# A macaron block on one core: both turn orders of the attention loop written anew, and four kinds of side work moved from VectorE to ScalarE and GpSimd

## The chip, the cores and the metric

The kernel runs on one core of a Trainium2 chip. The metric is the device time of one execution in microseconds (us). The core's engines run at the same time, each through its own list of instructions, in order: TensorE (PE: matmuls and transposes, with its weight loads shown as PEld), VectorE (DVE), ScalarE (ACT), GpSimd (POOL) and SyncE (SP, which here only issues DMAs). They wait for each other on semaphores.

## What is computed

The input x has 2 batches of 1024 rows and 512 columns, all in float32. Three residual steps follow each other:

```python
x = x + 0.5 * ffn(layernorm(x), W_base, b_base, W_router, lora_A, lora_B)
x = x + attn(layernorm(x), q_weight, q_scale, ..., o_weight, o_scale)
x = x + 0.5 * ffn(layernorm(x), W_base, b_base, W_router, lora_A, lora_B)

def ffn(x):      # base layer, and a low-rank part: 8 experts of rank 16, the best 2 weighted
    w = weights of the top 2 of softmax(x @ W_router.T)
    h = einsum('td,erd->ter', x, lora_A)
    return x @ W_base.T + b_base + 2 * einsum('ter,eor,te->to', h, lora_B, w)

def bitnet_linear(x, weight, scale):
    s = max(mean(abs(weight), axis=1), 1e-8)
    y = (x @ sign(weight / s).T) * (s * scale)
    return nan_to_num(y, nan=0, posinf=1e6, neginf=-1e6)

def attn(x):     # 32 query heads of 16, 8 key and value heads
    q, k, v = bitnet_linear(x, ...) three times
    a = softmax(q @ k.T / 4)
    return bitnet_linear(a @ v, o_weight, o_scale)
```

## The kernel before

The attention is the trunk of the program. It is cut into 32 units (a batch, half of its 1024 queries, one of the 8 key heads with its 4 query heads), and a unit into 4 turns. One turn issues, for three units at different stages:

- m: 8 score tiles of 128 queries by 512 keys, two matmuls each (p = 0 and 1, line 742), and for each tile a row maximum on VectorE (`m_max`, line 751);
- e: 8 score tiles of 128 keys by 512 queries of an earlier unit, three matmuls each (lines 781 and 785; the third subtracts the maximum), and for each tile the exponential on ScalarE into one of 14 `es` buffers (line 787);
- A: four parts of the product of exponentials and values (`a_part`, line 820), one turn behind e. All parts of a unit add up in one PSUM bank, `av`, of which there is only one. After the unit's last part, `unit_end` has ScalarE copy `av` out (line 795).

An m or e matmul uses 32 of the array's 128 rows, those of its head, which is the tile's number modulo 4. Four that follow each other with four different heads run at once. The order of m, e and A in a turn is written by hand: `FULL` and `BARE` (line 663 on), and `LEAD_IN` for the first three turns. `e1(6)` means matmul p = 1 of e tile 6, `A2` part 2. Seven PSUM banks are shared by m tiles, e tiles and all the rest; the bank that has been free longest is taken first.

The rest (layer norms, both FFNs, projections) is written as "strands": Python generators that yield the engine and the wait of their next step. Nothing of this exists when the kernel runs; it only decides in which order the instructions are recorded. A turn counts as 64 ticks. At the slots `F`, `V`/`W`, `C`/`D` of the order a ready strand may record one step on TensorE (`P`), VectorE (`v`) or ScalarE (`a`), after every item one on GpSimd (`g`) and one on SyncE (`d`). `LATER` says how many ticks a step has to wait after the step that it depends on. A turn takes `FULL` when a P step will be ready by tick 40, else `BARE`, which has no `F`. One P step is, for example, one of four column chunks of an FFN base tile, four of the eight matmuls of an output tile, or four transposes. In the loop before, 97 turns are `FULL`, 32 `BARE` and 3 `LEAD_IN`. Before a unit's q and k are loaded (`place`) or its v is laid out (`place_v`), `need` makes sure that the projections which feed them have been recorded: it lets the strands record step after step, with no attention work between them, until they are there.

Steps that the change touches, while the attention runs (`flow.free` is False then; before and after the loop it is True):

- `finite` (line 227) replaces infinities and NaN: with `fast` = 0 GpSimd clamps (249, 253) and adds (255), VectorE makes the mask (251) and copies the finite values over (259).
- `ln_T` (267): GpSimd makes `rstd` (281), VectorE the normalized rows `xn` (288), TensorE transposes them, ScalarE copies.
- `ffn_tiles`, in it `base` (410): GpSimd makes `xb` = x + half the bias (414), TensorE adds up five chunks (419, 423), VectorE writes 0.5 times the sum plus `xb` to x (425); then the store, or the statistics of the next norm (`stats`, 264).
- `o_proj` (617): VectorE multiplies the projection by the scales (639), then `finite`, then GpSimd adds to x (645).

Of the kernel before, what the change touches and what calls it, by code (L numbers as in the profile page):

```python
# [8 lines left out]
F32 = mybir.dt.float32  # L9
# [3 lines left out]
ALU = mybir.AluOpType  # L13
AX = mybir.AxisListType

P = 128
# [16 lines left out]
def macaron_kernel(ctx: ExitStack, tc: tile.TileContext, x_in, wbT, b_base, wrT, aT, bT,  # L33
# [192 lines left out]
    def finite(y, o, n, fast, back):  # L226
# [20 lines left out]
        else:  # L247
            yield "g", src, t
            nc.gpsimd.tensor_scalar(lo_, y, 0.0, -BIG, ALU.min, ALU.max)  # L249
            yield "v", src, t  # L250
            nc.vector.tensor_scalar(m_, y, 0.0, 0.0, ALU.mult, ALU.is_equal)
# [18 lines left out]
    def ln_T(xt, n, mv, given, tiles, xs, rank):  # L270
# [10 lines left out]
        nc.gpsimd.tensor_tensor(rstd[:, own], ve[:, own], mhalf[:, own], ALU.pow)  # L281
        at = flow.t

        def part(t):
            yield "r", dict(t=1)
            yield "v", "g", at
            xn = t512(f"xn{n}_{t}")
            nc.vector.tensor_scalar(xn, xt[:, t, :], mv[:, t, 0:1], rstd[:, t:t + 1], ALU.subtract,
                                    ALU.mult)
            yield "P", "v", None, 1  # L290
            pt = bank(f"pt{n}_{t}").rearrange("p (c q) -> p c q", c=KC)
            for c in range(KC):
                nc.tensor.transpose(pt[:, c, :], xn[:, c * P:(c + 1) * P], ident)
            flow.give(t=1)
            yield "a", "P"
            tok = slice(t * P, (t + 1) * P)
            nc.scalar.copy(xT[:, :, tok], pt)
            if xL is not None:
                yield "v", "a"
                nc.vector.tensor_tensor(xL[:, :, tok], pt, xT[:, :, tok].bitcast(F32), ALU.subtract)  # L300
            flow.give(fb=1)
# [18 lines left out]
    def ffn_tiles(xt, name, rank, tiles, xT, hT, mv, given, mv2, summed, store, loads):  # L320
# [89 lines left out]
        def base(t):  # L410
            yield "r", dict(t=1)
            yield "g", ""
            xb = t512(f"xb{n}_{t}")
            nc.gpsimd.tensor_tensor(xb, xt[:, t, :], bh, ALU.add)
# [9 lines left out]
            yield "v", "P"  # L424
            nc.vector.scalar_tensor_tensor(xt[:, t, :], pb, 0.5, xb, ALU.mult, ALU.add)
            flow.give(t=1, fb=1)
            if store is not None:
                yield ("a" if flow.free else "d"), "v"
                (nc.scalar if flow.free else nc.sync).dma_start(store[t * P:(t + 1) * P, :],
                                                                xt[:, t, :])  # L430
            if mv2 is not None:
                yield "v", "v"
                stats(xt, t, mv2, n)
                summed.add(t)
# [184 lines left out]
    def o_proj(b, g, hs, rank, mv, given, fast=False):  # L619
# [5 lines left out]
        def part(t):  # L625
# [11 lines left out]
            yield "v", "P"  # L637
            y = t512(f"yo{n}_{t}")
            nc.vector.tensor_tensor(y, po, osc, ALU.mult)  # L639
            flow.give(fb=1)  # L640
            done.append(t)
            r = t512(f"ro{n}_{t}")
            yield from finite(y[:, :], r[:, :], f"o{n}_{t}", fast, ("v", flow.t))
# [8 lines left out]
        for t in range(TG):  # L652
# [10 lines left out]
    FULL = ("e0(3) e0(2) m0(5) m0(0) e1(3) e1(2) m1(5) V m1(0) e2(3) e2(2) C e0(1) A0 A1 A2 A3 S "  # L663
            "m0(1) m0(6) e0(7) e0(4) m1(1) m1(6) e1(7) W e1(4) e1(1) m0(2) e2(7) e2(4) e2(1) C "
            "m1(2) V F e0(6) e0(0) m0(7) e0(5) e1(6) e1(0) m1(7) e1(5) e2(6) e2(0) D m0(3) e2(5) "
            "m0(4) m1(3) F m1(4)")
    BARE = ("C m0(1) m0(2) e0(3) e0(4) V m1(1) e0(6) e1(3) e1(4) m0(5) e1(6) e2(4) e2(3) m1(5) "
            "m1(2) A0 S e2(6) e0(1) m0(0) e0(7) e1(1) C m1(0) e1(7) W m0(6) e2(1) e0(0) e2(7) m1(6) "
            "A1 e1(0) V m0(7) e0(5) e0(2) e2(0) D m1(7) e1(2) e1(5) m0(4) m0(3) e2(2) e2(5) m1(4) "
            "m1(3) A2 A3")  # L670
# [4 lines left out]
         for o in t.split()] for t in (FULL, BARE, LEAD_IN))  # L675
    TU = NT // 2
# [154 lines left out]
    def attention(chains, n0):  # L831
# [7 lines left out]
        def need(*keys):  # L839
            for _ in range(4000):  # L840
                flow.settle()
                if set(keys) <= ended:
                    return
# [6 lines left out]
        for n in range(n0, TU * len(units) + LEAD + 1):  # L850
# [8 lines left out]
            order = (LEAD_IN if not e and not a else FULL if flow.wants("P", begin + TICK * 5 // 8)  # L859
# [3 lines left out]
            for pos, (kind, p, i) in enumerate(order):  # L863
# [7 lines left out]
                elif kind == "A":  # L871
                    if a:
                        a_part(a[0], a[1] * 2 + p // 2, p % 2)
# [149 lines left out]
```

## Time and profile before

| | |
|---|---|
| median of 3 runs | 1261.95 us (1256.4 to 1266.83) |
| the profiled execution: time, span of its instructions | 1256.92 us, 1255.2 us |
| mean granted TensorE clock | 0.915 of full speed |
| the loop over turns, first matmul of its first turn to first matmul of its last | 118.4 to 1183.5 us |
| row maximum, line 751, VectorE | 1024 x 682 ns |
| exponential, line 787, ScalarE | 1024 x 599 ns |
| m matmuls, line 742; e matmuls, lines 781 and 785 | 2048 x 464 ns; 2048 x 474 ns and 1024 x 431 ns |
| A matmuls, line 820, each float32 one in two passes | 4096 x 416 ns |
| FFN base, line 419, the same | 256 passes, 68.9 and 64.8 us in all |

Durations of matmuls overlap, so their sum is not TensorE's time; what counts there is the distance from one start to the next. Each row of 40 digits on the page cuts the span in slices of 31.4 us; a digit is the busy share in tenths. Where `PEclk` has an 8 or a 7 the array ran at half speed for part of the slice.

### The profile page before, as it was taken

What the parts mean: (1) busy time and instruction counts of PE and PEld (TensorE: products, weight loads), DVE (VectorE), ACT (ScalarE), POOL (GpSimd) and SP (SyncE); (2) the same over time, 40 slices, a digit from 0 to 9 for tenths busy, and PEclk for the clock granted to TensorE, in tenths of its full rate; (3) what the DMA queues carried; (4) which work ended last, traced back from release to release, by engine and by line L of the source; (5) the groups of instructions that cost most, each with busy time, mean ns of one, the idle gap of its engine ahead of it and who ended that gap; (6) DMA issues with size and microseconds to landing.
All of it is one profiled execution on the core that took longest, in us unless ns stands there. A gap on an engine that the chain in (4) does not pass through costs nothing.

```text
span 1255.2 us, 25499 instructions
## 1 busy us (share of the span) xinstructions
PE 1148.8 (92%) x10501; PEld 606.1 (48%) x10501; DVE 902.8 (72%) x1733; ACT 641.6 (51%) x1249; POOL 295.0 (24%) x302
## 2 busy tenths in 40 slices
PE   3988699999999999999999999999999999998868
PEld 3546355454454544444554445444455444545434
DVE  5578876767786777776677976777769677895273
ACT  2222255655554665565565666455557655566401
POOL 3135832000000340031555220241000300422110
PEclk8989588899986999987999899899989899999788
DMA  7010332121212222223132241122222422211110
GB/s 254 1 59 34 81 122 85 52 52 52 52 52 52 69 80 57 70 76 89 49 90 75 72 122 53 33 52 69 61 60 67 123 68 65 68 55 38 45 39 34
DMA packets 38708, 85.57 MB, mean 68 GB/s; under 512 B 7728, under 2 KB 10800, under 8 KB 34624
## 3 DMA queue, kind: packets, MB, share of 16 engines
q1 hardware_dynamic: 37184, 81.26, 22.4%
q8 instruction: 82, 1.34, 0.4%
q10 hardware_dynamic: 1152, 2.10, 0.4%
q0 software_dynamic: 256, 0.59, 0.3%
q14 instruction: 34, 0.28, 0.1%
HBM read 59.57 MB, written 23.84 MB: 66 GB/s over the span
## 4 chain that ended last, share of the span: by engine, by line
PE 70%; DVE 19%; issue 3%; DMA 2%; POOL 2%; ACT 1%; SPq 1%; POOLq 0%; ACTq 0%; DVEq 0%
PE av L820 20%; PE m L742 16%; DVE mn L751 11%; PE e L781 10%; PE pbf L419 5%; PE pbs L419 5%; PE e L785 4%; PE po L634 2%; PE phs L342 1%; DMA qd<-y 1%; PE pq L504 1%; PE pbf L423 1%; PE pv L521 1%; PE pbs L423 1%; DMA x<-in_x 1%
## 5 line engine op out<-in xcount | busy, mean ns | idle before, releaser
L751 DVE TENSOR_REDUCE mn<-m 128x1 f32<-128x512 f32 x1024 | 657.0, 682 | 230.0 <-PE m L742 221.4
L787 ACT ACTIVATE es<-e 128x512 f32<-128x512 f32 x1024 | 546.9, 599 | 425.6 <-PE e L785 401.4
L742 PE MATMUL m<-k,q 32*128 32x512 f32 x2048 | 492.1, 464 | 21.1 <-DVE mn L751 15.1
L781 PE MATMUL e<-q,k 32*128 32x512 f32 x2048 | 407.9, 474 | 8.3 <-DVE mn L751 6.9
L742 PEld LDWEIGHTS m<-k,q 32*128 32x128 f32 x2048 | 240.8, 196 | 153.0 <-issue 67.4
L820 PE MATMUL av<-es,vaug 128*32 128x256 f32 x4096 | 290.3, 416 | 16.4 <-issue 10.3
L781 PEld LDWEIGHTS e<-q,k 32*128 32x128 f32 x2048 | 185.1, 194 | 114.7 <-DVE mn L751 69.6
L785 PE MATMUL e<-mq,ones_r 2*128 2x512 f32 x1024 | 233.0, 431 | 3.7 <-DMA mq<-mT 3.7
L820 PEld LDWEIGHTS av<-es,vaug 128*32 128x32 f32 x4096 | 121.5, 116 | 154.5 <-issue 103.8
L785 PEld LDWEIGHTS e<-mq,ones_r 2*128 2x128 f32 x1024 | 125.6, 196 | 25.1 <-issue 13.7
L419 PE MATMUL pbf<-wb,xTf 128*128 128x512 f32 x128 | 68.9, 653 | 1.3 <-DVE mn L751 1.3
L419 PE MATMUL pbs<-wb,xTs 128*128 128x512 f32 x128 | 64.8, 618 | 1.2 <-DVE mn L751 1.2
L586 POOL TENSOR_TENSOR an<-an,rb 128x512 f32<-128x512 f32 x15 | 19.2, 1281 | 142.7 <-DMA rd<-rs 72.1
L249 POOL TENSOR_SCALAR loa<-y 128x512 f32<-128x512 f32 x17 | 12.7, 750 | 157.1 <-ACT y L509 147.5
L726 POOL MEMSET vaug<- 128x128 f32 x32 | 6.6, 206 | 137.7 <-PE av L820 137.6
L419 PEld LDWEIGHTS pbf<-wb,xTf 128*128 128x128 f32 x128 | 23.2, 203 | 30.1 <-issue 26.1
L419 PEld LDWEIGHTS pbs<-wb,xTs 128*128 128x128 f32 x128 | 21.5, 189 | 27.1 <-issue 22.9
L253 POOL TENSOR_SCALAR z<-y 128x512 f32<-128x512 f32 x17 | 34.1, 2008 | 1.8 <-DMA qd<-y 0.6
L249 POOL TENSOR_SCALAR loo<-yo 128x512 f32<-128x512 f32 x12 | 7.4, 613 | 113.7 <-DVE yo L639 110.0
L537 POOL TENSOR_TENSOR z<-z,y 128x512 fp32r<-128x512 f32 x17 | 21.9, 1293 | 51.0 <-ACT y L534 51.0
L590 POOL TENSOR_TENSOR anxL<-an,anxT 128x512 fp32r<-128x512 f32 x15 | 19.2, 1280 | 53.5 <-ACT anxT L588 53.4
L634 PE MATMUL po<-sign_o,anxT 128*128 128x512 f32 x64 | 29.4, 459 | 1.2 <-DVE mn L751 1.2
(193 smaller groups left out, 1008.3 us busy)
## 6 DMA issues: line engine op xcount, KB each, us to landing
k<-kd SPq DMA_DIRECT2D x31, 1024.0 KB
q<-qd SPq DMA_DIRECT2D x32, 256.0 KB
ad<-avs SPq DMA_DIRECT2D x32, 256.0 KB
x<-in_x SPq DMA_DIRECT2D x16, 256.0 KB
qd<-y SPq DMA_DIRECT2D x16, 256.0 KB
qd<-z SPq DMA_DIRECT2D x16, 256.0 KB
an<-ad SPq DMA_DIRECT2D x15, 256.0 KB
rb<-rd SPq DMA_DIRECT2D x15, 256.0 KB
```

The costliest lines, as they stand in the source:

```text
L249: nc.gpsimd.tensor_scalar(lo_, y, 0.0, -BIG, ALU.min, ALU.max)
L253: nc.gpsimd.tensor_scalar(o, y, 0.0, BIG, ALU.max, ALU.min)
L419: nc.tensor.matmul(pb, xT[:, c, t * P:(t + 1) * P], wb[:, c, :], start=(c == 0), stop=False)
L423: nc.tensor.matmul(pb, hT[0][:, t * P:(t + 1) * P], lb, start=False, stop=True)
L537: (nc.vector if fast else nc.gpsimd).tensor_tensor(lo, o, y, ALU.subtract)
L634: nc.tensor.matmul(po, hs[j][:, c, t * P:(t + 1) * P], wo[:, c, :], start=(c + j == 0), stop=(c + j == KC))
L742: nc.tensor.matmul(s["m", i], s["q"][rows, qt * P:(qt + 1) * P], s["k"][rows, 1 - p, kh * 512:(kh + 1) * 512], start=(p == 0), stop=(p == 1))
L751: nc.vector.tensor_reduce(s["mn"][:, h, qt, kh:kh + 1], s.pop(("m", i)), AX.X, ALU.max, negate=True)
L781: nc.tensor.matmul(t, s["k"][rows, 1 - p, kt * P:(kt + 1) * P], s["q"][rows, :], start=(p == 0), stop=False)
L785: nc.tensor.matmul(t, ones_r[two, :], s["mq"][two, :], start=False, stop=True)
L787: nc.scalar.activation(e, s.pop(("e", i)), AF.Exp, scale=HD ** -0.5)
L820: nc.tensor.matmul(s["av"][32 * h:32 * h + 32, cols], s["v"][:, kt, :], s["es"][kt * REP + h][:, cols], start=(kt + half == 0), stop=(kt + ...
```

## The change

It does five things.

1. `FULL` and `BARE` are new orders of the same 44 attention items. In `FULL` the four A parts, which stood together at places 13 to 16 of 53, are now two pairs, one after the first eleven e and m items, one at the very end. In `BARE` they were one, one and two; now they are one, two and one, the last at the end. `at_F`, the tick by which a P step must be ready for `FULL` to be taken, goes from 40 to 36.
2. Before a unit's first A part, `until` now lets strands record steps until the copy of the previous unit's `av` has been recorded.
3. In `finite` with `fast` = 0 the mask (251) is made by GpSimd.
4. While the attention runs, `ln_T` makes `xn` on ScalarE from `rstd` and a new `neg` = -mean x rstd, for which GpSimd gets two small operations a group of tiles.
5. While the attention runs, FFN sums leave PSUM through a ScalarE copy with the factor 0.5 and are added to x by GpSimd, and output tiles leave through a ScalarE copy and are multiplied by the scales on GpSimd. The bias is now added to x in place in all cases.

Counted in the built program: VectorE loses 28 `xn`, 33 masks, 16 FFN sums and 12 scalings, 89 operations. ScalarE gains 28, 16 and 12, GpSimd 33, 16 and 12 of 128x512 and 16 of 128x4 or less. 91 turns are now `FULL`, 38 `BARE`, 3 `LEAD_IN`. The number of matmuls stays, and so does the number of DMAs.

```diff
@@ -247,8 +247,8 @@
         else:
             yield "g", src, t
             nc.gpsimd.tensor_scalar(lo_, y, 0.0, -BIG, ALU.min, ALU.max)
-            yield "v", src, t
-            nc.vector.tensor_scalar(m_, y, 0.0, 0.0, ALU.mult, ALU.is_equal)
+            yield "g", ""
+            nc.gpsimd.tensor_scalar(m_, y, 0.0, 0.0, ALU.mult, ALU.is_equal)
             yield "g", ""
             nc.gpsimd.tensor_scalar(o, y, 0.0, BIG, ALU.max, ALU.min)
             yield "g", "g"
@@ -279,15 +279,26 @@
         yield "g", "v"
         rstd = sm.tile([P, TG], F32, tag="rstd", name=f"rstd{n}{tiles[0]}", bufs=4)
         nc.gpsimd.tensor_tensor(rstd[:, own], ve[:, own], mhalf[:, own], ALU.pow)
+        calm = not flow.free
+        if calm:
+            yield "g", ""
+            neg = sm.tile([P, TG], F32, tag="neg", name=f"neg{n}{tiles[0]}", bufs=4)
+            nc.gpsimd.tensor_tensor(neg[:, own], mv[:, own, 0], rstd[:, own], ALU.mult)
+            yield "g", ""
+            nc.gpsimd.tensor_scalar(neg[:, own], neg[:, own], -1.0, None, ALU.mult)
         at = flow.t
 
         def part(t):
             yield "r", dict(t=1)
-            yield "v", "g", at
+            yield "a" if calm else "v", "g", at
             xn = t512(f"xn{n}_{t}")
-            nc.vector.tensor_scalar(xn, xt[:, t, :], mv[:, t, 0:1], rstd[:, t:t + 1], ALU.subtract,
-                                    ALU.mult)
-            yield "P", "v", None, 1
+            if calm:
+                nc.scalar.activation(xn, xt[:, t, :], AF.Identity, bias=neg[:, t:t + 1],
+                                     scale=rstd[:, t:t + 1])
+            else:
+                nc.vector.tensor_scalar(xn, xt[:, t, :], mv[:, t, 0:1], rstd[:, t:t + 1],
+                                        ALU.subtract, ALU.mult)
+            yield "P", "a" if calm else "v", None, 1
             pt = bank(f"pt{n}_{t}").rearrange("p (c q) -> p c q", c=KC)
             for c in range(KC):
                 nc.tensor.transpose(pt[:, c, :], xn[:, c * P:(c + 1) * P], ident)
@@ -410,8 +421,7 @@
         def base(t):
             yield "r", dict(t=1)
             yield "g", ""
-            xb = t512(f"xb{n}_{t}")
-            nc.gpsimd.tensor_tensor(xb, xt[:, t, :], bh, ALU.add)
+            nc.gpsimd.tensor_tensor(xt[:, t, :], xt[:, t, :], bh, ALU.add)
             for c in range(KC):
                 yield ("P", "P") if c else ("P", "", flow.t, 1)
                 if c == 0:
@@ -421,15 +431,24 @@
                 flow.lock = bs[t] if c < KC - 1 else None
             yield "P", "a", ready
             nc.tensor.matmul(pb, hT[0][:, t * P:(t + 1) * P], lb, start=False, stop=True)
-            yield "v", "P"
-            nc.vector.scalar_tensor_tensor(xt[:, t, :], pb, 0.5, xb, ALU.mult, ALU.add)
-            flow.give(t=1, fb=1)
+            if flow.free:
+                yield "v", "P"
+                nc.vector.scalar_tensor_tensor(xt[:, t, :], pb, 0.5, xt[:, t, :], ALU.mult, ALU.add)
+                flow.give(t=1, fb=1)
+            else:
+                yield "a", "P"
+                hb = t512(f"hb{n}_{t}")
+                nc.scalar.activation(hb, pb, AF.Copy, scale=0.5)
+                flow.give(fb=1)
+                yield "g", "a"
+                nc.gpsimd.tensor_tensor(xt[:, t, :], xt[:, t, :], hb, ALU.add)
+                flow.give(t=1)
             if store is not None:
-                yield ("a" if flow.free else "d"), "v"
+                yield ("a" if flow.free else "d"), "v" if flow.free else "g"
                 (nc.scalar if flow.free else nc.sync).dma_start(store[t * P:(t + 1) * P, :],
                                                                 xt[:, t, :])
             if mv2 is not None:
-                yield "v", "v"
+                yield "v", "v" if flow.free else "g"
                 stats(xt, t, mv2, n)
                 summed.add(t)
 
@@ -634,13 +653,19 @@
                     nc.tensor.matmul(po, hs[j][:, c, t * P:(t + 1) * P], wo[:, c, :],
                                      start=(c + j == 0), stop=(c + j == KC))
                 flow.lock = ss[t] if c < 2 else None
-            yield "v", "P"
+            yield "v" if fast else "a", "P"
             y = t512(f"yo{n}_{t}")
-            nc.vector.tensor_tensor(y, po, osc, ALU.mult)
+            if fast:
+                nc.vector.tensor_tensor(y, po, osc, ALU.mult)
+            else:
+                nc.scalar.copy(y, po)
             flow.give(fb=1)
             done.append(t)
+            if not fast:
+                yield "g", "a"
+                nc.gpsimd.tensor_tensor(y, y, osc, ALU.mult)
             r = t512(f"ro{n}_{t}")
-            yield from finite(y[:, :], r[:, :], f"o{n}_{t}", fast, ("v", flow.t))
+            yield from finite(y[:, :], r[:, :], f"o{n}_{t}", fast, ("v" if fast else "g", flow.t))
             yield "v" if fast else "g", "v"
             (nc.vector if fast else nc.gpsimd).tensor_tensor(xt[:, t, :], xt[:, t, :], r, ALU.add)
             flow.give(t=2)
@@ -660,19 +685,20 @@
 
 
 
-    FULL = ("e0(3) e0(2) m0(5) m0(0) e1(3) e1(2) m1(5) V m1(0) e2(3) e2(2) C e0(1) A0 A1 A2 A3 S "
-            "m0(1) m0(6) e0(7) e0(4) m1(1) m1(6) e1(7) W e1(4) e1(1) m0(2) e2(7) e2(4) e2(1) C "
-            "m1(2) V F e0(6) e0(0) m0(7) e0(5) e1(6) e1(0) m1(7) e1(5) e2(6) e2(0) D m0(3) e2(5) "
-            "m0(4) m1(3) F m1(4)")
-    BARE = ("C m0(1) m0(2) e0(3) e0(4) V m1(1) e0(6) e1(3) e1(4) m0(5) e1(6) e2(4) e2(3) m1(5) "
-            "m1(2) A0 S e2(6) e0(1) m0(0) e0(7) e1(1) C m1(0) e1(7) W m0(6) e2(1) e0(0) e2(7) m1(6) "
-            "A1 e1(0) V m0(7) e0(5) e0(2) e2(0) D m1(7) e1(2) e1(5) m0(4) m0(3) e2(2) e2(5) m1(4) "
-            "m1(3) A2 A3")
+    FULL = ("e0(2) e0(7) e0(1) m0(4) e1(2) e1(7) e1(1) m1(4) e2(2) e2(7) V e2(1) A0 S D A1 e0(0) "
+            "e0(6) m0(1) m0(3) C e1(0) e1(6) m1(1) m1(3) W e2(0) e2(6) e0(5) V F e1(5) e0(3) m0(0) "
+            "m0(6) e2(5) e1(3) m1(0) m1(6) F C m0(7) e0(4) m0(5) m0(2) m1(7) e1(4) m1(5) m1(2) "
+            "e2(3) e2(4) A2 A3")
+    BARE = ("m0(5) e0(3) e0(0) m1(5) e1(3) m0(2) e1(0) e2(3) m1(2) m0(1) e2(0) e0(7) A0 S e0(5) "
+            "e1(7) V V e0(2) C m1(1) e2(7) e1(2) m0(4) e1(5) m0(7) m1(4) e2(2) e2(5) m1(7) W A1 A2 "
+            "m0(0) e0(6) e0(1) m1(0) e1(6) D m0(3) e1(1) e0(4) C e2(6) e1(4) m0(6) e2(1) m1(3) "
+            "e2(4) m1(6) A3")
     LEAD_IN = ("m0(0) m0(5) m0(2) V m1(0) m1(5) F C V m0(7) m1(2) m1(7) V F C m0(4) m0(1) m0(6) V m1(4) "
                "m1(1) F C V m0(3) V m1(6) S m1(3) F C V")
     FULL, BARE, LEAD_IN = (
         [(o[0], int(o[1]) if len(o) > 1 else 0, int(o[3]) if len(o) > 2 else 0)
          for o in t.split()] for t in (FULL, BARE, LEAD_IN))
+    at_F = TICK * FULL.index(("F", 0, 0)) // len(FULL)
     TU = NT // 2
     LEAD = TU + 1
     units = [(b, qb, g) for b in range(B) for qb in range(NQB) for g in range(G)]
@@ -837,9 +863,12 @@
         live = []
 
         def need(*keys):
+            until(lambda: set(keys) <= ended)
+
+        def until(cond):
             for _ in range(4000):
                 flow.settle()
-                if set(keys) <= ended:
+                if cond():
                     return
                 flow.t += 1
                 for kind in "Pvagd":
@@ -856,7 +885,7 @@
             if e and e[1] == 0:
                 need(*[(units[e[0]][0], h, KC + 1) for h in range(NG)])
                 place_v(e[0])
-            order = (LEAD_IN if not e and not a else FULL if flow.wants("P", begin + TICK * 5 // 8)
+            order = (LEAD_IN if not e and not a else FULL if flow.wants("P", begin + at_F)
                      else BARE)
 
             hold = n % TU == 0 and n // TU
@@ -870,6 +899,8 @@
                         e_tile(e[0], e[1] * 2 * REP + i, p)
                 elif kind == "A":
                     if a:
+                        if a[0] and a[1] == p == 0:
+                            until(lambda: "av" not in st[a[0] - 1])
                         a_part(a[0], a[1] * 2 + p // 2, p % 2)
                 elif kind == "S":
                     if 0 < hold <= len(units):
```

## The prediction, made before the changed kernel had run

> **What bounds the kernel now.** I read the page first: shares of the engines, the clock's row, the chain that ended last.
>
> ```profile
> span 1255.2 us, 25499 instructions
> PE 1148.8 (92%) x10501; PEld 606.1 (48%) x10501; DVE 902.8 (72%) x1733; ACT 641.6 (51%) x1249; POOL 295.0 (24%) x302
> PEclk8989588899986999987999899899989899999788
> PE 70%; DVE 19%; issue 3%; DMA 2%; POOL 2%; ACT 1%; SPq 1%; POOLq 0%; ACTq 0%; DVEq 0%
> ```
>
> TensorE leads, VectorE holds a fifth of the chain, ScalarE and GpSimd nearly nothing. The work is moved to the engines with room, which is for it. But the average hides the turns, so the windows view came next, cut at the first matmul of a turn:
>
> ```profile
> core 0: us, PE busy (x) PEld busy (x) DVE busy (x) ACT busy (x) POOL busy (x), PEclk, DMA share, GB/s
> 501.84:509.17 7.33, 7.33 (x78) 3.48 (x77) 6.10 (x11) 4.22 (x9) 0.00 (x0) 1.00 0.01 2
> 269.27:345.47 76.20, 75.03 (x771) 36.19 (x770) 55.86 (x95) 43.67 (x84) 0.44 (x2) 1.00 0.17 46
> 695.66:725.32 29.66, 29.56 (x365) 15.14 (x361) 28.42 (x54) 22.10 (x41) 7.17 (x7) 0.97 0.33 85
> 735.79:742.61 6.82, 6.82 (x74) 3.06 (x73) 5.20 (x9) 5.43 (x11) 1.28 (x1) 1.00 0.34 103
> ```
>
> First the shortest kind of FULL turn with two base steps, 7.33 us; then ten FULL turns, 7.62 each, VectorE busy 5.6 of it: TensorE's. Then five BARE turns, 5.93 each, VectorE busy 5.68: VectorE's (eight maxima alone are 8 x 0.682 = 5.46). Last, one BARE turn between FULL ones: 6.82, so going from FULL to BARE costs about 0.9.
>
> Then the timeline at a place where the chain says "issue" for 1.76 us, a unit boundary reached from a BARE turn, whose last A part stands at its end:
>
> ```profile
> 725.90 0.39 PE L781 MATMUL e<-q,k 32*128 32x512 f32 x1
> 725.90 0.40 PE L785 MATMUL e<-mq,ones_r 2*128 2x512 f32 x2
> 726.40 1.08 ACT L787 ACTIVATE es<-e 128x512 f32<-128x512 f32 x2 [0.90 <-PE e L785]
> 727.37 0.59 ACT L795 COPY avs<-av 128x512 f32<-128x512 f32 x1
> 728.06 0.66 PE L820 MATMUL av<-es,vaug 128*32 128x256 f32 x4 [1.76 <-issue]
> ```
>
> The next unit's first A part needs the only `av` bank, whose copy stands on ScalarE behind two exponentials of e tiles issued just before. TensorE, in order, stands from 726.30 to 728.06. The distance 725.90 to 728.06 is 2.16, against 0.33 where nothing is missing (502.56 to 502.89 in the turn of 7.33): 1.8 lost. Seven of the 31 boundaries look like this; after a FULL turn the parts lie in the first third of the turn and the copy has a whole turn.
>
> **The change part by part.**
>
> *Unit boundaries.* In the new FULL order parts A2 and A3 are last, and in 21 of the first 30 boundaries the next turn is FULL: e2(2), e2(7), e2(1) come before A0, so three exponentials and the copy do. A third exponential adds 0.49 (their starts lie 0.49 apart in the trace): 2.65, less 0.33, is 2.32 lost. The built program's order shows what a strand gets in between, as `until` lets it: a base step (two passes, 1.06) at ten boundaries, leaving 1.26; four output matmuls (1.0; eight take 2.04 in the chain) at four, leaving 1.3; a short step (about 0.5) at five, leaving 1.8; nothing at two, 2.32. At nine the next turn is BARE: two exponentials, one four-wide group (0.24) earlier: 1.58. Sum 12.6 + 5.2 + 9.0 + 4.6 + 14.2 = 45.6; less 7 x 1.77 = 12.4 in the old order: **+33**. Cover: in FULL turns none, TensorE is the bound; bounds +20 to +45.
>
> *The clock after a stall.* The windows view on the old stalls:
>
> ```profile
> 667.80:669.90 2.10, 0.42 (x7) 0.02 (x1) 1.88 (x4) 1.56 (x3) 0.46 (x1) 1.00 0.50 145
> 669.90:673.40 3.50, 3.48 (x32) 1.79 (x32) 0.03 (x1) 0.00 (x0) 3.33 (x3) 0.51 0.47 179
> 757.40:759.50 2.10, 0.41 (x7) 0.03 (x1) 1.29 (x2) 1.56 (x3) 0.00 (x0) 1.00 0.52 121
> 759.50:762.90 3.40, 3.40 (x49) 2.20 (x50) 0.77 (x2) 0.52 (x2) 0.00 (x0) 1.00 0.23 84
> ```
>
> Of five stalls that began at full clock, two (669.9 and 728.0) were followed by 3.4 us at half clock, three were not. The Trainium skill (TensorE: Matmul & The Clock Gate, "Why this matters for your kernels") asks for no idle gap over about 3 us; by it gaps of 2.1 cost 0. The trace disagrees in two of five. At 2 in 5 for the eleven bare stalls and 1 in 5 for the nineteen shortened ones, less the two there were, 6 more drops, 1.7 us each (half of 3.4): **+10**; ends 0, and 41 if all 24 further boundaries drop.
>
> *The order of FULL.* Steps from the turn of 7.33: four-wide groups start 0.34, then 0.23 apart; into A 0.33, each of its eight passes 0.215, out 0.33; a base pass 0.53. Both orders need 11 such groups, but the new one breaks them four times instead of three, 0.3 for leaving and re-entering. Against it: when a strand holds banks, the old order waits about 0.6 for a bank at its last tile before A (its FULL turns are 7.33 or about 7.97); the new one has its own, since the maximum of m0(5), issued late in the turn, frees the bank for e0(1) at the start of the next, about 0.2. That makes some 7.7 against 7.62 to 7.68: +0.1 x 91 = **+9**; bounds -15 and +30.
>
> *The order of BARE.* Counted by heads, 13 groups instead of 11 and again three breaks: 0.47 more for TensorE, by the same steps 5.26 to 5.73. VectorE drops to its 5.46 and a rest, so TensorE takes over at nearly the same time: -0.1 x 38 = **-4**; bounds -15, +10. FULL-to-BARE passages go from 19 to 15 and the two orders now end alike; half of 19 x 0.9: **-9**; bounds 0, -19.
>
> *VectorE's 89 operations.* 28 x 0.63 + 33 x 0.63 + 16 x 0.68 + 12 x 0.68 = 57 us. In FULL turns they lie beside TensorE; those in BARE turns are counted above. What remains are the output-projection turns, where VectorE is busy 7.5 to 8.3 of turns of 7.5 to 8.3; each of 12 tiles loses 1.36 there and half counts: **-8**; bounds 0, -16. ScalarE gains 56 x 0.6 = 34 us, 0.25 a turn, beside 4.8 of exponentials in turns of 5.7 or more: 0; where three such steps meet in a BARE turn (4.8 + 1.8) up to 0.9.
>
> *GpSimd.* A mask there is not in the trace; nearest are the two clamps, in the groups view 613 to 750 ns (line 249) and 1920 to 2008 (253). I take their mean, 1.33; adds are 1.3. In all 33 x 1.33 + 28 x 1.3 + 16 small ones (about 0.5) = 88 us on an engine busy 295. It matters where VectorE waits for it. (a) The first turns: between 120 and 160 us GpSimd is busy 32 of 40, and 9 masks add 12 to chains that end in VectorE's copy (259) and in the loads of q and k: **+6**, between 0 and 12. (b) Turn 60. There `need` asks for the second batch's keys. In the old program strands are nearly there: 24 matmuls are forced, GpSimd has 12 operations, the turn is 12.7. In the new one, longer chains are further behind: the order shows 4 + 32 + 24 matmuls forced (1.0 + 3.9 + 6.1 = 11.0), and on VectorE, ahead of the first maximum of turn 61, eight copies (259), the last one behind 32 GpSimd operations: 42 us. TensorE has work for 7.7 + 11.0 and some 5 of turn 61 until no bank is free, 24; it then stands about 19. The old turn wasted some 4, and a restart at half clock costs 2: **+17**; bounds +5 and +25. (c) Late output tiles: five to six GpSimd operations a turn are 7 to 8 us, in BARE turns of 6, with copies (259) behind them: **+3**, 0 to 10.
>
> *Queues.* Stores of the last FFN, still on SyncE, now wait for GpSimd; behind them stand q and k loads, issued four turns (30 us) ahead: 0, a few us if GpSimd is that late. `stats` waits for GpSimd too, in strands that have turns to spare.
>
> Sum: 33 + 10 + 9 - 4 - 9 - 8 + 6 + 17 + 3 = +57. On the profiled execution's 1257 that is **1314**, where the runs shown have their median 5 higher; I say 1315.
>
> **The rivals.**
>
> *Faster.* VectorE's shorter list removes the bank waits: FULL goes to 7.33 (-0.3 x 91), BARE to 5.5 (-0.43 x 38), passages cost nothing (-17), -8 as above: -69, against +33, +17, +6, and the 3 of (c): 1257 - 10 = 1247, and less if turn 60 is milder: 1240. For it: FULL turns vary by 0.6 from bank waits alone. Against: a fourth break is in the order itself. It decides from a mean FULL turn under 7.3.
>
> *Nearly the same.* Stalls at boundaries are made good, since ScalarE and VectorE catch up in them and the turns after run without waits: +33 and +10 shrink to 15, the rest stays: about 1286; with the FULL order at its good end 1270.
>
> *Slower still.* Each stall drops the clock (+41 instead of +10), and turn 60 takes its whole 25: 1315 + 39, about 1355. For it: one stall was followed at once by the drop; against: three of five were not.
>
> *The change doesn't do what it says:* if the FULL and BARE orders did not fit, `until` would force more than one step at a boundary; the built order shows one at most.
>
> **How the numbers follow.** Forecast 0.55 (1290 to 1335), nearly the same 0.2, slower still 0.15, faster 0.1. About 1% is what a measurement here can tell from no change. Below 1249: 0.1; 1249 to 1275: 0.12; above: 0.78. The range 1260 to 1360 leaves out the faster case and the end of the slow one.
>
> **What would show it.** At unit boundaries, three exponentials, the copy, and an A matmul with 1 to 2.3 us of idle before it, some 30 times; a gap of about 20 us in TensorE and VectorE in turn 60, GpSimd busy throughout; more digits of 8 in the clock's row; the mean FULL turn at 7.6 to 7.8. I am wrong if FULL turns are under 7.4, if the copy comes ahead of the exponentials, or if GpSimd ends turn 60's list within 25 us.

## The result, and the profile after

| | before | after |
|---|---|---|
| median | 1263.53 us (1255.97 to 1277.07, 6 runs) | 1314.88 us (1305.11 to 1350.59, 6 runs) |
| profiled execution: time, span | 1256.92, 1255.2 | 1322.17, 1320.2 |
| granted clock, mean | 0.915 | 0.904 |

The change makes the kernel slower: ratio 1.04, 95% interval 1.0359 to 1.044. (Executions of one kernel fall into a faster and a slower group; medians are of all of them, ratios and intervals of the faster ones alone, so a ratio need not be the quotient of two medians.) The page of the changed kernel: span, engines, clock row, shares of the chain that ended last.

```profile
span 1320.2 us, 25611 instructions
...
PE 1170.4 (89%) x10501; PEld 600.1 (45%) x10501; DVE 868.3 (66%) x1644; ACT 680.0 (52%) x1305; POOL 397.1 (30%) x379
...
PEclk8998599999989999989598959999889999997589
...
PE 78%; DVE 8%; POOL 6%; issue 4%; ACT 2%; DMA 2%; SPq 0%; POOLq 0%; ACTq 0%; DVEq 0%
```

VectorE is relieved as meant (903 to 868 us busy, 19% to 8% of the chain). But TensorE's idle time grew from 106 us (1255.2 - 1148.8) to 150, and GpSimd, which was 2% of the chain, is 6%: 295 us of work became 397. The clock row has three holes that were not there: the 20th slice, the 24th, and the 37th and 38th.

Where the 65 us of span went, cut at the first matmul of a turn. "Idle" is the length less TensorE's busy time in the windows view; "half" is the time in which the clock record shows half speed.

| turns | before: us, idle, half | after: us, idle, half | difference |
|---|---|---|---|
| before turn 2 | 118.4, 26.6, 17 | 117.7, 27.9, 14 | -0.7 |
| 2 to 9 | 82.8, 17.9, 53 | 76.3, 16.9, 41 | -6.5 |
| 10 to 59 | 413.9, 18.8, 66 | 414.1, 20.3, 34 | +0.2 |
| 60, 61 | 22.7, 1.8, 2 | 58.3, 26.3, 34 | +35.6 |
| 62 to 127 | 509.3, 19.6, 42 | 519.8, 24.2, 68 | +10.5 |
| 128, 129 | 11.9, 0, 0 | 15.8, 0, 0 | +3.9 |
| 130 to the end | 96.1, 21.5, 32 | 118.3, 34.1, 61 | +22.2 |

Two short places, turns 60 and 61 and what comes from turn 130 on, hold nearly all of it. The hundred and more turns between, with their 30 unit boundaries, come out only 11 us longer.

A unit boundary, in the timeline of the changed kernel (start, length, engine, line; in brackets the idle time before the group and its releaser):

```profile
461.50 0.60 PE L811 MATMUL e<-mq,ones_r 2*128 2x512 f32 x3
...
461.94 1.57 ACT L813 ACTIVATE es<-e 128x512 f32<-128x512 f32 x3 [0.77 <-PE e L811]
462.02 1.12 PE L433 MATMUL pbf<-lb,hTf 128*128 128x512 f32 x2
...
463.38 0.61 ACT L821 COPY avs<-av 128x512 f32<-128x512 f32 x1
...
464.09 0.85 PE L846 MATMUL av<-es,vaug 128*32 128x256 f32 x12 [0.94 <-issue]
```

Three exponentials stand on ScalarE ahead of the copy; `av` is free 0.1 us before A0 starts. A short step (L433) hides part of the wait. From the start of the last matmul pass before A0 to A0 itself it is 1.15 to 2.61 us at all of the first 30 boundaries, where before it was over 2 at seven and under 0.6 at the rest. Less the 0.33 of a boundary without a wait, these distances sum to 40.1 us, against 12.7 before (distances under 0.6 left out). The expectation of x35 below says 45.7: that starts at the first pass of a float32 matmul, and so counts 5.6 us in which its second pass runs.

Turns 60 and 61, and turn 130 with the stretch behind it, in the windows view of the changed kernel:

```profile
core 0: us, PE busy (x) PEld busy (x) DVE busy (x) ACT busy (x) POOL busy (x), PEclk, DMA share, GB/s
608.10:626.46 18.36, 18.36 (x147) 12.97 (x143) 11.07 (x19) 6.45 (x12) 17.33 (x13) 1.00 0.01 2
626.46:666.37 39.91, 13.57 (x81) 6.87 (x80) 11.58 (x16) 7.57 (x14) 35.80 (x26) 0.57 0.10 28
1201.91:1223.59 21.68, 8.27 (x60) 3.38 (x56) 11.31 (x29) 5.25 (x14) 6.17 (x5) 0.56 0.11 36
1223.59:1247.90 24.31, 24.31 (x124) 10.12 (x124) 0.00 (x0) 9.87 (x20) 0.00 (x0) 0.50 0.00 1
```

In the second row TensorE works 13.6 of 39.9 us and GpSimd 35.8: GpSimd is what the others wait for. The waits of turns 60 and 61 say so link by link (who waited <- for whom: us in total, times, longest):

```profile
ACT y L553 <- DVE z L259: 25.8, 3, 14.4
DVE z L259 <- POOL z L255: 21.8, 4, 5.8
...
PE m L768 <- ACT es L813: 15.6, 1, 15.6
...
PE e L807 <- DVE mn L777: 9.5, 1, 9.5
```

ScalarE's cast waits for VectorE's copy of finite values, which waits for GpSimd; TensorE stands 15.6 and 9.5 us since exponentials and maxima are queued behind those on their engines.

The end, turn 130, in the changed kernel's timeline. The last unit's normalization reads `av` itself with two reciprocals, and the next unit's A0 needs the second one:

```profile
1205.35 1.75 DVE L832 RECIPROCAL avr<-av 128x256 f32<-128x256 f32 x1
...
1207.48 4.95 POOL L424 TENSOR_TENSOR x<-x,bh 128x512 f32<-128x512 f32 x4
...
1211.28 1.19 DVE L401 TENSOR_TENSOR w_s<-w_s,w_s 128x16 f32<-128x16 f32 x1
...
1214.08 0.18 DVE L401 TENSOR_TENSOR w_s<-w_s,w_s 128x16 f32<-128x16 f32 x1
...
1214.64 1.75 DVE L832 RECIPROCAL avr<-av 128x256 f32<-128x256 f32 x1
1216.53 1.08 PE L846 MATMUL av<-es,vaug 128*32 128x256 f32 x8 [13.41 <-DVE avr L832]
```

The `until` before A0 waits for the strand to get there and lets other strands record steps meanwhile: a whole routing (L392 to L404) lands on VectorE between the two reciprocals. A0 waits 13.4 us; before, it waited 3.6 at this boundary.

### The profile page after: what moved, and what is told of

It reads as the page before. It is cut to its first block, busy times and chain, and to the rows that moved or that the text cites. A ratio compares the mean times of both kernels' runs of the same rounds, so it can differ in the third digit from the quotient of the medians.

```text
span 1320.2 us, 25611 instructions
## 1 busy us (share of the span) xinstructions
PE 1170.4 (89%) x10501; PEld 600.1 (45%) x10501; DVE 868.3 (66%) x1644; ACT 680.0 (52%) x1305; POOL 397.1 (30%) x379
## 4 chain that ended last, share of the span: by engine, by line
PE 78%; DVE 8%; POOL 6%; issue 4%; ACT 2%; DMA 2%; SPq 0%; POOLq 0%; ACTq 0%; DVEq 0%
PE av L846 21%; PE e L807 17%; PE m L768 14%; PE e L811 6%; PE pbf L429 4%; PE pbs L429 4%; PE po L653 2%; PE pq L523 2%; DVE mn L777 2%; POOL ma L251 1%; ACT es L813 1%; PE phs L353 1%; PE pbf L433 1%; POOL z L253 1%; DMA x<-in_x 1%
## 5 line engine op out<-in xcount | busy, mean ns | idle before, releaser
L768 PE MATMUL m<-k,q 32*128 32x512 f32 x2048 | 447.2, 467 | 35.0 <-ACT es L813 20.0
L807 PE MATMUL e<-q,k 32*128 32x512 f32 x2048 | 465.5, 475 | 13.0 <-DVE mn L777 10.6
L846 PE MATMUL av<-es,vaug 128*32 128x256 f32 x4096 | 311.9, 415 | 49.8 <-issue 33.2
L807 PEld LDWEIGHTS e<-q,k 32*128 32x128 f32 x2048 | 221.0, 196 | 167.6 <-issue 69.2
L768 PEld LDWEIGHTS m<-k,q 32*128 32x128 f32 x2048 | 209.1, 195 | 137.2 <-DVE mn L777 52.6
L811 PE MATMUL e<-mq,ones_r 2*128 2x512 f32 x1024 | 252.9, 419 | 2.0 <-DMA mq<-mT 2.0
L846 PEld LDWEIGHTS av<-es,vaug 128*32 128x32 f32 x4096 | 107.9, 114 | 209.2 <-issue 173.6
L605 POOL TENSOR_TENSOR an<-an,rb 128x512 f32<-128x512 f32 x15 | 19.6, 1307 | 181.7 <-DMA rb<-rd 179.7
L553 ACT CAST y<-z 128x512 fp32r<-128x512 f32 x20 | 12.4, 621 | 62.6 <-DVE z L259 59.5
L249 POOL TENSOR_SCALAR loa<-y 128x512 f32<-128x512 f32 x17 | 13.5, 796 | 93.9 <-ACT y L528 93.2
L424 POOL TENSOR_TENSOR x<-x,bh 128x512 f32<-128x512 f32 x32 | 40.7, 1299 | 0.0
L259 DVE COPY_PREDICATED z<-ma,y 128x512 f32<-128x512 uint8 x20 | 19.2, 958 | 30.8 <-POOL z L255 30.7
L429 PEld LDWEIGHTS pbf<-wb,xTf 128*128 128x128 f32 x128 | 22.8, 199 | 27.7 <-issue 26.6
```

The source lines that it names most:

```text
L424: nc.gpsimd.tensor_tensor(xt[:, t, :], xt[:, t, :], bh, ALU.add)
L429: nc.tensor.matmul(pb, xT[:, c, t * P:(t + 1) * P], wb[:, c, :], start=(c == 0), stop=False)
L605: nc.gpsimd.tensor_tensor(z, z, rb, ALU.mult)
L768: nc.tensor.matmul(s["m", i], s["q"][rows, qt * P:(qt + 1) * P], s["k"][rows, 1 - p, kh * 512:(kh + 1) * 512], start=(p == 0), stop=(p == 1))
L807: nc.tensor.matmul(t, s["k"][rows, 1 - p, kt * P:(kt + 1) * P], s["q"][rows, :], start=(p == 0), stop=False)
L811: nc.tensor.matmul(t, ones_r[two, :], s["mq"][two, :], start=False, stop=True)
```

## The experiments

Thirteen profiles were cut into the same stages. "Idle" and "half" below are of turns 10 to 59 and 62 to 127 together (before 38.5 and 108, after 44.5 and 102; their length 923.2 and 933.9). Ratios are to the kernel before in runs on the same chip.

**The two halves of the change, each alone.** x1_old_orders is the changed kernel with the old turn orders and their tick:

```diff
-    FULL = ("e0(2) e0(7) e0(1) m0(4) e1(2) e1(7) e1(1) m1(4) e2(2) e2(7) V e2(1) A0 S D A1 e0(0) "
+    FULL = ("e0(3) e0(2) m0(5) m0(0) e1(3) e1(2) m1(5) V m1(0) e2(3) e2(2) C e0(1) A0 A1 A2 A3 S "
...
-            order = (LEAD_IN if not e and not a else FULL if flow.wants("P", begin + at_F)
+            order = (LEAD_IN if not e and not a else FULL if flow.wants("P", begin + TICK * 5 // 8)
```

> The moved work alone: FULL, BARE and the tick that chooses them are those of before, the rest is the changed kernel. Theory 1 (the new orders carry the loss, through the copy of av behind three exponentials at unit boundaries): stalls of about 1.8 us return only at boundaries reached from a BARE turn, as before (7 or so). The forced turn 60 stays, with 26 GpSimd operations recorded in it instead of 36, some 15 us over the kernel before; VectorE's relief gives back 15 to 25. Together 1245 to 1265 us. Rival (the moved work itself slows the turns, through GpSimd and ScalarE): 1285 us or more, with FULL turns above 7.9 us on average.

x2_old_engines is the kernel before with the new orders, `at_F` and the `until` before A0, nothing moved:

```diff
+                        if a[0] and a[1] == p == 0:
+                            until(lambda: "av" not in st[a[0] - 1])
```

> The new orders alone, with all strand work on its old engines. No turn forces a long list at turn 60 here; the last units still do at turn 130. Theory 1: some 30 boundaries with an idle TensorE before the unit's first A matmul, +33 us; the turns at the end +15 to +20; nothing at turn 60: 1300 to 1320 us. Rival (boundary stalls are made good in the turns after, the loss is turn 60's): 1265 to 1280 us.

x1: 1273.51 us, ratio 1.01 (1.0043 to 1.0157). x2: 1279.82, ratio 1.0143 (1.0075 to 1.0211). So each half alone costs 1 to 1.5%, and together they cost 4%. x1 fell between its two forecasts: boundaries waited 5.2 us, but turns 60 and 61 took 41.7, so the moved work makes a gap there by itself, 19 of the 36 us. The orders alone make none: 13.7 in x2. x2's time came out at the end of the rival's range, but not for the rival's reason. Its boundaries waited 39.3, 26.6 more than before, and its turns 10 to 59 and 62 to 127, with nearly the same strand work (656 passes of matmuls for 652), took 34.9 more (958.1): nothing is made good there. Turns 2 to 9 and 60, 61 took 4.7 and 9.0 less, and the end 9.2 more.

**The two short places.** x4_hurry uses the fast form of `finite` while `need` forces steps; x5_tail lets both reciprocals read the copy, so `av` is free after it:

```diff
+        fast = fast or flow.hurry
...
+            flow.hurry = not set(keys) <= ended
```

> The changed kernel, but parts whose clamps are recorded while turn 60 forces the strands make them and the mask on VectorE (one GpSimd operation a part instead of four; 21 GpSimd operations in the turn instead of 36, 39 on VectorE instead of 25). Theory (GpSimd's list of some 42 us, which the first maximum of turn 61 stands behind, sets the gap): turns 60 and 61 fall from 58.3 us to about 35, the time by 15 to 25, to 1290 to 1300. Rival (the gap is made by ScalarE's casts or by loads): turns 60 and 61 stay above 50, the time within 5 of 1314.

```diff
-                yield "v", "P" if j == 0 else "v"
-                nc.vector.reciprocal(r[:, cols], st[u]["av"][:, cols])
-                if j == 1:
-                    st[u].clear()
+                yield "v", "a" if j == 0 else "v"
+                nc.vector.reciprocal(r[:, cols], o[:, cols])
```

> The changed kernel, but the reciprocals of the last two units read the copy of av instead of av itself, so that the bank is free after the copy, as at every other boundary. Theory (turn 130 waits for the second reciprocal, behind the routing operations that until recorded ahead of it): turn 130 falls from 21.7 us to about 9, the half clock of the turns after it goes at least in part, and the time falls by 12 to 22, to 1293 to 1303. Rival (the end is slow because its turns have no score tiles and the clock drops anyway): the time falls by no more than 5.

x4: 1304.81 us, ratio 1.0322 (1.0243 to 1.0402), less of a gain than expected; turns 60 and 61 fell from 58.3 to 39.3, half of the excess. (Turns 10 to 59 and 62 to 127, with as many matmuls as in the changed kernel, took 940.6 in this execution, with 126 us at half clock: so far can two profiles lie apart.) x5: 1302.90, ratio 1.0317 (1.0248 to 1.0385); from turn 130 on 118.3 became 100.2, and every other stage stayed within 1 us of the changed kernel's. That settles the tail: 18 of its 22 us are the reciprocals' wait.

**The boundary wait taken away.** The wait for the copy is moved from just before A0 to the start of the turn, so the copy is recorded ahead of the turn's exponentials. x35 is the changed kernel with this and x5's edit; x10 the same two edits on x2, x7h on x1 (with x4's edit), x9 on the kernel before. That is a table of orders by engines without boundary waits.

```diff
+            if a and a[0] and a[1] == 0:
+                until(lambda: "av" not in st[a[0] - 1])
             hold = n % TU == 0 and n // TU
...
-                        if a[0] and a[1] == p == 0:
-                            until(lambda: "av" not in st[a[0] - 1])
```

> The changed kernel with two edits: the copy of av is recorded at the start of the turn, ahead of the turn's exponentials, instead of just before A0; and the tail fix of x5_tail. Its built order forces nothing at turns 60 or 129 (99 FULL and 30 BARE turns). Theory (the stalls before A0 are lost time, 45.7 over 30 boundaries, and turn 60 costs some 40 because strands fell behind): boundary idle falls to under 10, turns 60 and 61 take 16 to 22 instead of 58, the tail 100 instead of 118, so 1315 - 40 - 38 - 18 = about 1220, range 1205 to 1240. Rival (stalls are mostly made good afterwards, by engines that catch up in them): only turn 60 and the tail come back, 1255 to 1265. A second rival: the copy at the start of the turn holds the turn's first exponentials up by 0.6 and the FULL turn grows by 0.3 to 0.6: also about 1255.

> The kernel before with the new FULL and BARE orders, the copy at the start of the turn and the tail fix, and nothing of the moved work (FULL 92, BARE 37). Against x2_old_engines (1280, the new orders alone) the boundaries give back 45: 1230 to 1240. If the moved work off VectorE is worth something once stalls and turn 60 are out of the way, x35 is below this by 10 to 20; if it is worth nothing, they agree within 6; if it costs, x35 is above. If stalls are made good: 1265 to 1280.

> The changed kernel with the old FULL and BARE orders and their tick, the copy at the start of the turn, the tail fix, and finite's fast path at turn 60 (x4_hurry's edit). Against x1_old_orders (1273): the boundaries had only 5 idle there, so 1273 less 5, less some 15 at turn 60: 1245 to 1258. If this equals x35, the new orders are worth nothing by themselves; the theory says that without stalls they are worth some 0.2 a turn, so x35 is below this by 20 or more.

> The kernel before with the copy at the start of the turn and the tail fix alone (old orders, old engines). Boundaries had 12.7 idle in it, half clock after them a few more; the tail hardly changes: 1259 - 13 - 0 to 8 = 1238 to 1248. With x10, x7h and x35 it makes a table of orders by engines without stalls: x10 - x9 and x35 - x7h are the worth of the orders, x7h - x9 and x35 - x10 that of the moved work. If copy first costs something itself (the first exponentials later), this one is at 1259 or above.

| copy first, and tail edit | work on the old engines | work moved |
|---|---|---|
| old orders | x9: 1255.55, ratio 0.9919 (0.9878 to 0.9959) | x7h: 1233.93, ratio 0.9771 (0.9725 to 0.9816) |
| new orders | x10: 1205.08, ratio 0.952 (0.9465 to 0.9576) | x35: 1197.77, ratio 0.9496 (0.9452 to 0.9541) |

x35 beats both kernels: 5% under before, 9% under the change, and 7 us under the lowest value of its forecast. x10 and x7h also came in lower than foreseen, x9 higher. The page of x35:

```profile
span 1196.3 us, 25646 instructions
...
PE 1116.4 (93%) x10501; PEld 573.2 (48%) x10501; DVE 862.3 (72%) x1642; ACT 678.5 (57%) x1307; POOL 398.5 (33%) x381
...
PEclk8999589999999899999999999999999999999969
...
PE 83%; DVE 8%; POOL 3%; DMA 3%; ACT 2%; issue 1%; SPq 1%; DVEq 0%; ACTq 0%; POOLq 0%
```

The same matmuls (x10501) keep TensorE busy 54 us less than in the changed kernel, and the clock row is full of nines. The same boundary in x35's timeline:

```profile
441.68 1.13 PE L429 MATMUL pbf<-wb,xTf 128*128 128x512 f32 x2
441.82 0.59 ACT L821 COPY avs<-av 128x512 f32<-128x512 f32 x1
...
443.30 0.40 PE L811 MATMUL e<-mq,ones_r 2*128 2x512 f32 x3
...
443.64 0.85 PE L843 MATMUL av<-es,vaug 128*32 128x256 f32 x12
443.74 0.60 ACT L813 ACTIVATE es<-e 128x512 f32<-128x512 f32 x1 [1.33 <-PE e L811]
```

The copy is done 1.2 us before A0, which starts without a wait, 0.33 after the matmul before it. In the windows view, turns 10 to 59, 60 and 61, 62 to 127, of x35 and then of the changed kernel:

```profile
192.10:581.60 389.50, 385.59 (x3955) 193.13 (x3953) 290.90 (x529) 253.88 (x481) 102.11 (x102) 0.99 0.25 69
581.60:597.50 15.90, 15.46 (x161) 8.09 (x161) 12.26 (x22) 10.21 (x21) 9.90 (x9) 1.00 0.28 72
597.50:1086.00 488.50, 484.52 (x5104) 242.18 (x5102) 379.96 (x691) 324.24 (x621) 171.85 (x165) 0.99 0.26 73
```

```profile
194.00:608.10 414.10, 393.84 (x3916) 195.50 (x3912) 288.99 (x525) 253.36 (x479) 90.12 (x94) 0.96 0.23 64
608.10:666.40 58.30, 31.96 (x227) 19.87 (x223) 22.68 (x35) 14.05 (x26) 53.13 (x38) 0.71 0.07 20
666.40:1186.10 519.70, 495.46 (x5044) 245.86 (x5040) 370.07 (x665) 321.17 (x609) 137.54 (x138) 0.93 0.25 69
```

Outside turns 60 and 61 the 56 us are 37 of idle (44.5 to 7.9) and 19 of busy time, with half clock down from 102 us to 20. Inside them 42 us go: with the copy first the planner makes 46 of the first turns FULL instead of 44, the strands are not behind, and nothing is forced at turn 60.

The profiled execution of x9 took 1275.54 us, 20 above its median, so its stages are not set beside the others.

**One edit, and the dose.** x3_copy_first is the changed kernel with the moved wait alone. x6_one and x6_two are x35 with the copy recorded behind one and behind two of the turn's exponentials:

```diff
+                    tops += p == 2
+                    if copy and tops == 2 and p == 2:
+                        until(lambda: "av" not in st[a[0] - 1])
```

(`tops == 3` in x6_two, or before A0 where BARE has only two.)

> The changed kernel with one edit only: the copy of av recorded at the start of the turn. Its built order forces nothing at turn 60, but 128 ticks of work at turn 129. If the copy's place alone is what makes the change slow, this is already well below the kernel before: x35's 1198 plus the tail that x5_tail showed (18), 1210 to 1225. If x35's gain came from both edits acting together, 1240 or more.

> x35 with the copy recorded behind the turn's first exponential. A dose: by the exponentials' 0.49 to 0.6, the FULL boundary that idles 0 with none ahead and about 1.8 with three should idle about 0.7 here, so some 15 to 20 over 30 boundaries. Lost time in full: 1198 + 17, plus about 10 for 96 forced ticks at turn 60 in its built order, 1215 to 1235. If short idles are made good: under 1212. The clock should hardly react: 0.7 in a window of 3.41 leaves TensorE 80% busy, where one window in four was followed by half clock, so half clock in turns 10 to 59 and 62 to 127 between 20 and 50.

> x35 with the copy recorded behind two exponentials (before A0 where BARE has only two). Otherwise the built order is that of x6_one. FULL boundaries idle about 1.2: 30 to 36 over 30 boundaries, so 15 to 18 above x6_one, and more half clock (40 to 70): 1235 to 1260. If idle is made good, it equals x6_one within 5.

| exponentials ahead of the copy | median, ratio to before | waits at 30 boundaries | turns 10-59 and 62-127: us, idle, half |
|---|---|---|---|
| none (x3_copy_first) | 1205.23, 0.9539 (0.947 to 0.9607) | 0.4 | 881.1, 7.8, 31 |
| none (x35) | 1197.77, 0.9496 (0.9452 to 0.9541) | 0.4 | 878.2, 7.9, 20 |
| one (x6_one) | 1230.64, 0.9753 (0.9682 to 0.9824) | 13.2 | 899.8, 19.5, 44 |
| two (x6_two) | 1261.92, 0.9948 (0.9914 to 0.9981) | 23.8 | 929.7, 27.9, 88 |
| up to three (the change) | 1314.88, 1.04 (1.0359 to 1.044) | 40.1 | 933.9, 44.5, 102 |

x3: one edit turns +4% into -5%, and a little under its forecast of 1210 to 1225; the two edits do not need each other. Of what it gains on the changed kernel, 53 us lie in these turns and 42 in turns 60 and 61 (15.8), where its order forces nothing. x6_one came where expected, x6_two 2 us above its range by the median and inside it by the ratio, both with shorter waits than forecast (13.2 and 23.8 for 15 to 20 and 30 to 36), and x6_two with more half clock. Both have the same FULL and BARE turns and the same matmuls in each stage, so they show what the waits cost: in the two profiles 10.6 us more of waiting makes these turns 29.9 us longer, 8.4 as idle and 21.5 as busy time, with 44 us more at half clock, half of which is 22. The profiled execution of x6_two lies 10 us above what its ratio gives (0.9948 x 1259.94 = 1253.4); by the ratios the two lie 25 apart. Either way a wait costs at least as much again through the clock. (Both force 96 ticks of steps at turn 60, some 14 us, which x35 does not.)

From x6_two to the change these turns grow by 4 us only (some 14 with those 10 taken off), while idle grows by 17. The change has 80 FULL turns in this stretch where x6_two has 85, each some 2 us longer than a BARE one, and 600 passes of strand matmuls where x6_two has 680; whether that is the whole of the rest stays open.

## Why the prediction was right, and where not

The forecast of 1315 stands against 1314.88, by the mechanism that it put first. The hit of the sum is luck: its base was the profiled 1257, under the median of 1263.53, and errors of both signs cancel in it.

*Boundaries, +33.* Right in kind: three exponentials, the copy, a waiting A0, 30 times. In size 40.1 for 45.6 new and 12.7 for 12.4 old, so +27. Boundaries with nothing or a base step in between came as reckoned; with four output matmuls they lost 3.9 for 5.2, with a short step 5.5 for 9.0.

*The rival "stalls are made good"* is false by the dose: from none to two exponentials every microsecond of waiting costs more than one.

*The clock, +10.* This term failed. The rate was near: in turns 10 to 59 and 62 to 127 the changed kernel has 12 stretches at half clock, and 9 of them begin within 2 us of an A0, where the forecast had 8. But a stretch lasts 8.5 us in the mean, not one window of 3.4; and the old kernel, which was charged with two drops, has 15 stretches, of which two belong to its seven waits. Cut along the record's own windows of 3.41 us between 125 and 1165 us, it has 41 full-clock windows in which TensorE was busy under 90%, and 13 of them were followed by half clock; after, 41 and 14. Half clock went from 108 to 102 us, not up, which is -3 for +10. I counted only boundary stalls as its cause; the old orders had as many poor windows from other waits, which are in no single row of the waits view. (With 126 in x4, one profile does not tell a rise of 20 from none.)

*FULL +9, BARE -4, passages -9, output turns -8.* Together with the +33 and +10 it made +31 for turns 10 to 59 and 62 to 127; they grew by 10.7. With +27 and -3 put in, some -14 is left for these four, where -12 stood. That is near, but by chance, for of two things in it the forecast had one too small and the other not at all. First, the old orders' waits for banks went: idle time in these turns elsewhere than before A0 fell from 26.5 to 8.1. Gaps of 0.2 to 0.5 us in TensorE between 120 and 1170 us were 61 before, 59 of them ended by a row maximum, and 22 after; with the work alone (x1) 50, with the orders alone (x2) 27, in x35 17. So this is the orders' doing. Second, work left these turns: 80 of them are FULL where 88 were, and 600 passes of strand matmuls stand in them where 652 did; turns 60 and 61 have 44 more. Read together with turn 60, 48 was forecast and 46.3 came.

The fourth break of four-wide groups costs nothing that shows: FULL turns at full clock, without the first of a unit, take 7.78 (before 7.80), BARE turns 5.89 (6.39). The worth of the orders, once the copy is first, is 1255.55 to 1205.08. The "faster" rival had a mechanism right (bank waits go) and its test wrong (a FULL turn under 7.3).

*VectorE's shorter list* is worth less than its 57 us: from x10 to x35 the ratio goes from 0.952 to 0.9496, with intervals that overlap. With the old orders it is 0.9919 to 0.9771, though x7h also has x4's edit and another mix of FULL and BARE turns. TensorE, busy 94% of the span in x10, is the bound, and VectorE's operations lie beside it.

*First turns, +6:* wrong in sign. They became 6.5 shorter, with half clock down from 53 to 41. Most of it goes with the orders: alone they give 78.1 us with 41 at half clock (x2), the work alone 81.8 with 55 (x1). In no pair of kernels that differ in the moved work did it make these turns longer, so the masks on GpSimd do not hold the first q and k up.

*Turn 60, +17:* +35.6. The mechanism was right, forced strands and VectorE behind GpSimd. Idle rose by 24.5, where 15 was forecast (19 less 4). One cause of that is the price of a mask, put between two rows at 1.33: L251 takes 1.93 in the median, like the dearer clamp (253, 1.92), so GpSimd gained 102 us, not 88. The other 11 us are busy time: the passes that are forced here and not in other turns, which the forecast foresaw and did not add, and the clock, which stood at half for 34 us (631.0 to 665.1). TensorE was busy in 9 of these, so that cost some 4.5, where 2 was put.

*Late output tiles, +3:* turns 128 and 129 took 3.9 more, but they hold 33 passes of strand matmuls where 17 stood; no run takes this apart.

*Not in the sum at all:* the end, +22. I followed the `until` through 30 boundaries and took the 31st to be like them; there it waits for VectorE's reciprocals, not for ScalarE's copy.

So 48 of the sum was 46, 6 was -6.5, 3 was 4, and 22 were missing: +65 in the profiled executions, +51 between the medians.

## What to carry to other kernels

When one buffer is handed from one stage to the next, look at what is recorded ahead of the instruction that frees it on its own in-order engine; moving that one copy ahead of three exponentials took the ratio from 1.04 to 0.954 here. A change that loses may hold a gain under one wait: undo the parts one by one, then take the wait away and keep the rest. Where `until` or a planner lets other work in while it waits, follow every place where it can wait, the last one too, and what lands in between.

## What was unexpected of the hardware

*The clock and its windows.* The stretches in the clock record are multiples of 3.41 us. Windows of the changed kernel, two at a boundary wait that lies across the edge of two clock windows, then one with a wait inside it and what followed:

```profile
460.33:463.74 3.41, 2.82 (x29) 1.12 (x17) 2.68 (x5) 2.64 (x6) 0.00 (x0) 1.00 0.48 113
463.74:467.15 3.41, 3.06 (x32) 1.41 (x32) 1.28 (x2) 1.32 (x3) 0.00 (x0) 1.00 0.38 134
753.90:757.31 3.41, 1.95 (x28) 0.90 (x20) 3.24 (x14) 2.45 (x5) 0.00 (x0) 1.00 0.53 130
757.31:791.44 34.13, 34.13 (x243) 16.22 (x239) 20.06 (x43) 15.49 (x31) 9.10 (x9) 0.50 0.26 70
```

Waits of 0.9 and 1.5 us: the first leaves both windows over 80% busy and the clock stays; the second leaves one at 57%, and half clock follows for ten windows, although TensorE is busy all through. Over the thirteen profiles, full-clock windows (between 125 and 1165 us) were followed by half clock in 139 of 397 cases where TensorE was busy under 90%, in 13 of 270 between 90 and 95%, and in 8 of 2747 above. Of the 397, those under 50% were followed by it in all 19 cases, from 50 to 65% in 40 of 55, from 65 to 90% in 80 of 323. So above half busy it is a chance, not a threshold; and a window can be made poor by several short waits as well as by one of 1.5 us.

*Small VectorE operations beside GpSimd.* In turn 130 the same 128x16 product (L401) takes 1.19 us beside a GpSimd add (L424) and 0.18 once GpSimd is done; L399 takes 1.12 against 0.18, L392 0.92 against 0.16. The four long ones end at 1208.76, 1210.00, 1211.24 and 1212.46, the four adds at 1208.74, 1209.97, 1211.21 and 1212.43: each waits for the end of an add. The Trainium skill (SBUF — State Buffer, "Who interferes with whom") says that a VectorE instruction with two SBUF inputs contends with a GpSimd instruction that reads SBUF, and that the port pair they share is an exclusive lock; this trace agrees, to 0.03 us. Here it adds some 3.7 us to the wait between the two reciprocals.

*GpSimd's prices.* Of three operations on the same 128x512 tile, L249 takes 0.61 us in the median, L251 (the mask) 1.93 and L253 1.92. Shape and engine alone do not give the price.
